# A deformable-convolution and attention kernel: one channel block of the first two chunks' depthwise taps as TensorE products, and TensorE's opening work in another order

## The chip, the cores and the metric

The kernel runs on one core of a Trainium2 chip. A core has five engines, each with its own queue of instructions: PE (TensorE, matrix products; its weight loads are listed as PEld), DVE (VectorE), ACT (ScalarE), POOL (GpSimd) and SP (SyncE, which only issues DMAs). Each engine takes its instructions strictly in order, and an instruction waits on semaphores that other engines and DMAs raise. The metric is the device time of one execution in microseconds (us); before the change the median of three runs is 3317.27 us.

## What is computed

Everything is float32. The input `x` has 2 images of 512 channels and 64x64 pixels. Two layers are added to it.

```python
x = x + _L0_conv_ref(_gn(x), ...)      # deformable convolution
x = x + _L1_conv_ref(_gn(x), ...)      # attention over all pixels, batch norm, relu

def _L0_conv_ref(x, ...):              # inp: x with the channels last
    xproj = inp @ in_w + in_b
    x1 = depthwise 3x3 convolution of x + dw_b
    x1 = gelu(layer norm over channels of x1)
    offset = x1 @ off_w + off_b
    mask = softmax((x1 @ mask_w + mask_b).reshape(N, H, W, G, P), -1)
    out = _dcnv3_core(xproj, offset, mask)   # 9 samples per group, bilinear, weighted by mask
    return out @ out_w + out_b
```

`_gn` is a group norm over 32 groups. The change lies in the first layer, nearly all of it in the work ahead of that layer's loop.

## The kernel before

The 512 channels are four blocks (`KB`) of 128 partitions. An image is eight chunks of 8 rows, 512 pixels; the two images make 16 chunks (`NSEQ`). The first layer is a software pipeline over these 16 chunks, in which each chunk passes four stages. Every stage is a Python generator, and each `yield` ends one step of it:

- `project(i)` (line 738) normalizes the chunk's rows with the group norm's scale and bias into the one buffer `xn` (ScalarE, line 762), multiplies them by `in_w` on TensorE (line 772, four tiles `pq` of 128 pixels), copies each tile out on ScalarE into `xj` (line 778, two buffers), and stores it with two DMAs on SP's queue (line 780) into the padded image `xt` in DRAM.
- `features(i)` (line 786) is the depthwise convolution, the layer norm and Gelu. Tap 1 of each channel block is written by ScalarE (line 798); the other eight taps of each block are added by VectorE, one instruction each (line 806). For chunks 0 and 1 the sum over the channels is taken by TensorE with a matrix of ones over four blocks (`p_mean`, line 822), once for the mean and once for the squares; VectorE subtracts (827), takes the reciprocal and scales (842, 843), ScalarE squares (832), takes the root (840) and Gelu (849). `xn` is one buffer, so the rows of chunk 1 can only be written when TensorE and VectorE have read those of chunk 0.
- `weights(i)` (line 857) makes offsets and masks: TensorE multiplies the features (`po`, line 866), VectorE adds the bias (`o`, line 871), ScalarE takes Exp (878), and VectorE builds the 5x5 window weights `aw` in 17 instructions (909, 914). ScalarE then copies `aw` into `at` (919), TensorE transposes it (928), and ScalarE copies it on.
- `sample(i)` (line 946) spreads the weights (`pb`, `bt`, lines 957 and 962), multiplies them with patches of `xt` (`pa`, line 976), which `fetch` (line 934) has loaded on SP's queue, applies `out_w` (`py`, line 996) and adds the input.

The order of all this on each engine is written out by hand. Everything stands under a manual schedule: a call such as `f0(8)` takes eight steps of a stage, and its instructions go to the engines' queues at that point. Ahead of the loop stands **the fill** (lines 1156 to 1213): chunk 0 through `project`, `features` and `weights`, chunk 1 through `project` and `features`, chunk 2 through `project` and the first seven steps of `features`, six of them taps. In it `p0`, `p1`, `p2` are the projections, `f0`, `f1`, `f` the features of chunks 0, 1 and 2, and `v` the weights of chunk 0. Three further pieces of work are placed among them:

- `border()` (line 695): sixteen stores of the negated bias into the border of `xt` for both images, on SP's queue.
- `more()` (line 1151): one step of `image_stats(1)` (line 703), the group-norm statistics of image 1. Its pieces of 256 KB are loaded on POOL's queue into three buffers (the two halves of `early`, and `xraw`; line 714), and a buffer is loaded again when VectorE has taken its statistic (line 727). The fill takes 13 steps, of which the first only loads; the rest of the steps follow in the loop.
- `products` (`value_weights`, line 1124): four products of weights that the second layer needs (line 1129), copied out by ScalarE into a buffer shared with `xj` and stored on SP's queue (line 1134).

After the fill come 14 calls of `period` (line 1025), which interleaves the stages of four chunks, and then `next_to_last` (line 1087) and `last_period`. The second layer, from line 1235, is not touched.

Of the kernel before, what the change touches and what calls it, by code (L numbers as in the profile page):

```python
# [10 lines left out]
F32 = mybir.dt.float32  # L11
I32 = mybir.dt.int32
AF = mybir.ActivationFunctionType
# [5 lines left out]
P = 128  # L19
NB = 2  # L20
C = 512
KB = C // P
H = W = 64
# [6 lines left out]
NP = 9  # L30
GP = G * NP
CH = 512
NCH = S // CH
ROWS = CH // W
# [484 lines left out]
WIN = W + 4  # L519
# [35 lines left out]
def window_path(  # L555
# [3 lines left out]
    nc = tc.nc  # L559
# [8 lines left out]
    wc_d = dram.tile([P, KB, C], F32, name="wvfc")  # L568
# [57 lines left out]
    with ExitStack() as l0:  # L626
# [68 lines left out]
        def border():  # L695
            for n in range(NB):
                for e in (0, 1, WIN - 2, WIN - 1):
                    nc.sync.dma_start(xt_d[n][e], edge[:WIN, :])
                    nc.sync.dma_start(xt_d[n][2 : H + 2, e, :], edge[:H, :])

        gn = {}

# [35 lines left out]
        def project(i):  # L738

            n, ch = divmod(i, NCH)  # L740
            sc, bi = gn[n]
            lo, hi = max(ch * ROWS - 1, 0), min(ch * ROWS + ROWS + 1, H)
            r0 = lo - (ch * ROWS - 1)
            raws = deque()

            def read(kb):
                if i < 3:
                    raws.append(img[kb][:, lo * W : hi * W].rearrange("p (r c) -> p r c", c=W))
                else:
                    t = io.tile([P, ROWS + 2, W], F32, name="raw", bufs=3)  # L750
                    nc.sync.dma_start(t[:, : hi - lo, :].rearrange("p r c -> p (r c)"), x_v[n, :, kb, lo * W : hi * W])
                    raws.append(t[:, : hi - lo, :])

            for kb in range(3):
                read(kb)
            yield
            if ch == 0:
                nc.gpsimd.memset(xn[:, :, 0, :], 0.0)
            if ch == NCH - 1:
                nc.gpsimd.memset(xn[:, :, ROWS + 1, :], 0.0)  # L760
            for kb in range(KB):
                nc.scalar.activation(  # L762
                    xn[:, kb, r0 : r0 + hi - lo, :], raws.popleft(),
                    AF.Identity, bias=bi[:, kb : kb + 1], scale=sc[:, kb : kb + 1],
                )
                if kb + 3 < KB:
                    read(kb + 3)
                yield
            for t in range(ROWS // 2):
                pq = ps.tile([P, C], F32, tag="mm", name="pq")  # L770
                for kb in range(KB):
                    nc.tensor.matmul(  # L772
                        pq, xn[:, kb, 1 + 2 * t : 3 + 2 * t, :].rearrange("p r c -> p (r c)"), in_w[:, kb, :],
                        start=(kb == 0), stop=(kb == KB - 1),
                    )
                yield
                xj = io.tile([P, C], F32, name="xj", bufs=2)
                nc.scalar.copy(xj, pq)
                for r in range(2):
                    nc.sync.dma_start(xt_d[n][2 + ch * ROWS + 2 * t + r, 2 : W + 2, :], xj[r * W : (r + 1) * W, :])  # L780
                yield

        feats = {}
        conv = cv.tile([P, KB, CH], F32, name="conv")

        def features(i):

            a = cv.tile([P, KB, CH], F32, tag="dT", name="conv1", bufs=2) if i == 1 else conv
            def tap_of(kb, tap):
                dy, dx = tap // 3, tap % 3 - 1  # L790
                acc = a[:, kb, :].rearrange("p (r c) -> p r c", c=W)
                src = xn[:, kb, dy : dy + ROWS, max(dx, 0) : W + min(dx, 0)]
                return acc[:, :, max(-dx, 0) : W + min(-dx, 0)], src, dw_w[:, kb, tap : tap + 1]


            for kb in range(KB):
                dst, src, wt = tap_of(kb, 1)
                nc.scalar.activation(dst, src, AF.Identity, bias=dw_b[:, kb : kb + 1], scale=wt)  # L798
                if i != 2 or kb == KB - 1:
                    yield  # L800
            fill = i < 2
            tot = None if fill else sm.tile([P, CH], F32, tag="tot", name="tot")
            for kb in range(KB):
                for tap in (0, 2, 3, 4, 5, 6, 7, 8):
                    dst, src, wt = tap_of(kb, tap)
                    nc.vector.scalar_tensor_tensor(dst, src, wt, dst, ALU.mult, ALU.add)  # L806
                    if tap < 8:
                        yield

                if not fill:  # L810
                    if kb == 0:
                        nc.gpsimd.dma_start(tot, a[:, 0, :])
                    elif kb < KB - 1:
                        nc.gpsimd.dma_start(tot, a[:, kb, :], accum_op=ALU.add)
                    else:
                        nc.vector.tensor_add(tot, tot, a[:, kb, :])
                yield
# [269 lines left out]
        def next_to_last(y, v, m, w):  # L1087

            y(3)
            w(8)  # L1090
            v(4)
            for steps, tiles in ((1, 2), (1, 2), (2, 1), (1, 0)):
                m(2)
                w(steps)
                y(tiles)
            for _ in range(4):
                m(2)
                w(2)
            w(5)
# [24 lines left out]
        def value_weights():  # L1124

            for cb in range(KB):
                pw = ps.tile([P, C], F32, tag="mm", name="pw")
                for kb in range(KB):
                    nc.tensor.matmul(
                        pw, wv[:, kb, cb * P : (cb + 1) * P], wf[kb], start=(kb == 0), stop=(kb == KB - 1)  # L1130
                    )
                t = io.tile([P, C], F32, tag="xj", name="wc_part", bufs=2)
                nc.scalar.copy(t, pw)
                nc.sync.dma_start(wc_d[:, cb, :], t)
                yield

        def output_bias():
# [13 lines left out]
        def more():  # L1151
            next(later, None)

        with tc.manual_schedule():
# [3 lines left out]
            p0()  # L1158
            for kb in range(KB):
                p0()  # L1160
                f0()
            for t in range(4):
                p0(2)
                f0(8)
            border()
            more()
            p1()
            for kb in range(KB):
                p1()
                f1()  # L1170
                if kb == 1:
                    next(products)
                    next(products)
            f0()
            f1(5)
            p1(4)
            f0()
            f1(11)
            f0()
            for _ in range(6):  # L1180
                more()
            p1(4)
            f0(3)
            f1(16)
            next(products)
            fetch(0, 0)
            fetch(0, 1)
            p2()
            v(4)
            for _ in range(3):  # L1190
                more()
            f1()
            v(2)
            f1()
# [3 lines left out]
            f1()  # L1198
            v()
            f()  # L1200
            for _ in range(3):
                more()
            v(3)
            p2(4)
            f1()
            v(4)
            f1(2)
            v(5)
            p2(4)
            next(products)  # L1210
            run(output_bias())
# [23 lines left out]
    with ExitStack() as l1, tc.manual_schedule():  # L1235
# [78 lines left out]
        with ExitStack() as inner:  # L1314
# [565 lines left out]
            for n in range(NB):  # L1880
# [3 lines left out]
                for i in range(NCH // 2):  # L1884
                    if 0 < i < 3 or n and i == 0:
                        k = i + 1 if i else 1
# [164 lines left out]
```

## Time and profile before

| | us |
|---|---|
| median of three runs (lowest, highest) | 3317.27 (3314.47, 3319.29) |
| the profiled execution's own time | 3313.12 |
| its span, first to last instruction | 3311.0 |
| busy in it: PE, PEld, DVE | 3147.5, 2263.1, 2729.3 |
| busy in it: ACT, POOL | 1342.3, 291.7 |
| mean granted TensorE clock | 0.985 |
| first tap of chunk 0 on VectorE (line 806) | starts at 38.14 |
| first tap of chunk 2 on VectorE (line 806) | starts at 141.91 |
| reciprocal of line 842, first and last of 16 | 85.8 and 1039.4 |

The profiled execution is one run of its own; all times of single instructions come from it and count from the start of its span. A line of a timeline gives the start, the duration, the engine, the source line, the operation, output and inputs with their sizes, how many such instructions are merged, and in brackets how long the engine had been idle before and what ended the wait. A product in float32 is two passes of TensorE, so the profile counts two matmuls for one in the code. A line of stretches gives the busy time of each engine in a window, then the granted clock of TensorE, the share of the DMA engines in use and the GB/s that they moved.

### The profile page before, as it was taken

The numbers are of one execution on the slowest core, as the hardware profiler recorded it, in microseconds if no ns is written. First come the engines' busy times: TensorE is split into PE (matmuls) and PEld (weight loads), VectorE is DVE, ScalarE is ACT, GpSimd is POOL, SyncE is SP. The second block draws the span as 40 slices with busy tenths as digits, with TensorE's granted clock in tenths as the row PEclk, the third lists the DMA queues.
The fourth block names the chain that finished last, engine by engine and source line by source line (L and its number), as shares of the span: only waits on it lengthen the run. The fifth ranks groups of instructions, "written<-read, shape, count | busy, mean of one in ns | idle before, by whom it ended". The sixth has DMA issues, their size and how long they took to land. (4 is left out here: it accounts for less than half of the span.)

```text
span 3311.0 us, 38406 instructions
## 1 busy us (share of the span) xinstructions
PE 3147.5 (95%) x14207; PEld 2263.1 (68%) x14207; DVE 2729.3 (82%) x3907; ACT 1342.3 (41%) x1848; POOL 291.7 (9%) x420
## 2 busy tenths in 40 slices
PE   4899999999999899999999999999999999999993
PEld 2455555555555667787787877887777787787782
DVE  7999999999998678986876977968897796886875
ACT  2678888888887533203113112023311202203114
POOL 1100000000000000001001011000001101001022
PEclk9999999999999999999999999999999999999996
DMA  7345543443444268758657677557667758648689
GB/s 240 120 119 156 152 124 113 138 150 109 120 137 140 93 243 277 213 165 234 194 172 207 202 205 202 198 187 252 225 209 202 205 181 235 198 161 235 197 320 370
DMA packets 241236, 629.06 MB, mean 190 GB/s; under 512 B 28528, under 2 KB 45552, under 8 KB 240016
## 3 DMA queue, kind: packets, MB, share of 16 engines
q1 hardware_dynamic: 177952, 413.37, 37.7%
q0 software_dynamic: 51936, 179.86, 20.7%
q10 hardware_dynamic: 11152, 33.30, 2.7%
q8 instruction: 114, 1.87, 0.2%
q14 instruction: 82, 0.67, 0.1%
HBM read 406.61 MB, written 124.91 MB: 161 GB/s over the span
## 5 line engine op out<-in xcount | busy, mean ns | idle before, releaser
L1572 PE MATMUL accy<-tt,v 128*128 128x256 f32 x1944 | 579.2, 380 | 0.7 <-DVE ct L1638 0.6
L1459 ACT ACTIVATE e<-pS 128x1024 f32<-128x1024 f32 x256 | 248.3, 1021 | 746.8 <-PE pS L1454 732.2
L1572 PE MATMUL accx<-e,v 128*128 128x256 f32 x1728 | 454.2, 385 | 0.0
L1572 PE MATMUL accy<-e,v 128*128 128x256 f32 x1728 | 443.5, 379 | 0.0
L1572 PEld LDWEIGHTS accy<-tt,v 128*128 128x128 f32 x1944 | 369.0, 190 | 53.4 <-DVE tt L1530 2.2
L806 DVE SCALAR_TENSOR_TENSOR conv<-xn,L_conv_dw_w_sb,conv 128x504 f32<-128x504 f32 (+1 forms) x512 | 376.8, 744 | 29.1 <-ACT conv L798 15.2
L1572 PEld LDWEIGHTS accx<-e,v 128*128 128x128 f32 x1728 | 320.9, 190 | 116.7 <-issue 77.6
L1572 PEld LDWEIGHTS accy<-e,v 128*128 128x128 f32 x1728 | 328.3, 190 | 44.7
L1530 DVE TENSOR_TENSOR tt<-tt,e 128x512 f32<-128x512 f32 x432 | 298.9, 692 | 14.8
L1529 DVE TENSOR_TENSOR tt<-e 128x256 f32<-128x256 f32 x432 | 180.9, 419 | 135.8 <-PE accy L1572 133.5
L1572 PE MATMUL accx<-tt,v 128*128 128x256 f32 x972 | 289.9, 380 | 1.3 <-DVE tt L1529 1.3
L976 PEld LDWEIGHTS pa<-bt,patch 96*128 96x128 f32 x2048 | 249.5, 196 | 57.2 <-issue 38.5
L976 PE MATMUL pa<-bt,patch 96*128 96x128 f32 x2048 | 253.4, 280 | 7.8 <-issue 4.2
L1454 PE MATMUL pS<-q,keys 64*128 64x512 f32 x1024 | 254.7, 615 | 0.3 <-DVE stats L1799 0.3
L962 ACT COPY bt<-pb 96x1024 f32<-96x1024 f32 x120 | 226.1, 2025 | 44.0 <-PE pb L957 44.0
L772 PE MATMUL pq<-in_w,xn 128*128 128x512 f32 x512 | 233.8, 599 | 4.3 <-ACT xn L762 4.3
L996 PE MATMUL py<-dT,L_conv_out_w_sb 128*128 128x512 f32 x512 | 230.1, 593 | 0.0
L1577 ACT COPY u<-accx 128x256 f32<-128x256 f32 x54 | 20.1, 372 | 478.6 <-PE accx L1572 475.9
L987 ACT COPY dT<-pa 32x256 f32<-32x256 f32 x496 | 179.5, 362 | 60.3 <-PE pa L976 51.6
L1572 PEld LDWEIGHTS accx<-tt,v 128*128 128x128 f32 x972 | 184.6, 190 | 27.7 <-DVE tt L1529 2.7
L866 PE MATMUL po<-om_w_pg,feat 128*128 128x432 f32 x512 | 201.9, 538 | 1.6 <-ACT feat L849 1.6
L996 PEld LDWEIGHTS py<-dT,L_conv_out_w_sb 128*128 128x128 f32 x512 | 95.5, 190 | 114.3 <-issue 107.4
(289 smaller groups left out, 4383.2 us busy)
## 6 DMA issues: line engine op xcount, KB each, us to landing
v<-wv SPq DMA_DIRECT2D x420, 448.0 KB
tot<-e POOLq DMA_DIRECT2D x160, 512.0 KB, 6.8
patch<-xt SPq DMA_DIRECT2D x256, 192.0 KB
wv<-vform SPq DMA_DIRECT2D x48, 512.0 KB
v<-ww SPq DMA_DIRECT2D x54, 448.0 KB
wv<-vsum SPq DMA_DIRECT2D x48, 384.0 KB
xt<-xj SPq DMA_DIRECT2D x128, 128.0 KB
res<-in_x SPq DMA_DIRECT2D x64, 256.0 KB
```

The costliest lines, as they stand in the source:

```text
L772: nc.tensor.matmul(pq, xn[:, kb, 1 + 2 * t : 3 + 2 * t, :].rearrange("p r c -> p (r c)"), in_w[:, kb, :], start=(kb == 0), stop=(kb == KB ...
L806: nc.vector.scalar_tensor_tensor(dst, src, wt, dst, ALU.mult, ALU.add)
L866: nc.tensor.matmul(po[:, : 3 * GP], f[:, kb, t * P : (t + 1) * P], om_w[:, kb].rearrange("p a k g -> p (a k g)"), start=(kb == 0), stop=(k ...
L962: copy(bt[:SN].rearrange("s g q d -> s d (g q)")[:, d0 : d0 + 4, :], pb[:SN])
L976: nc.tensor.matmul(pa[:, p], xp[:SN, p, cb * P : (cb + 1) * P], bt[:SN, 4 * cb : 4 * cb + 4, PX * s + p, :], start=True, stop=True,)
L987: copy(dst, src)
L996: nc.tensor.matmul(py, out_w[:, kb, cb * P : (cb + 1) * P], dT[:, kb, :], start=(kb == 0), stop=(kb == KB - 1))
L1454: nc.tensor.matmul(p[:, a, :], keys[r, i, (2 * u + h) * P : (2 * u + h + 1) * P], c.q[r, qh, :], start=True, stop=True,)
L1459: nc.scalar.activation(e.rearrange("p a q -> p (a q)"), p.rearrange("p a q -> p (a q)"), AF.Exp)
L1529: nc.vector.tensor_sub(t[:, 0], x[:, 1], x[:, 3])
L1530: nc.vector.tensor_add(t[:, 1:3], t[:, 0].unsqueeze(1).to_broadcast([P, 2, HQ]), x[:, 0:3:2])
L1572: nc.tensor.matmul(out, v[:, blk, :], op, start=(first and g == 0), stop=(final and g == NG))
```

## The change

1. For chunks 0 and 1, the last channel block's nine taps leave ScalarE and VectorE. ScalarE makes nine diagonal matrices of the taps (`diagonals`), and TensorE sums nine products of these with shifted windows of `xn` in one PSUM tile (`deep`); ScalarE copies the tile to `conv` and adds the bias. Chunk 2 and all later chunks keep their taps as they were.
2. `deep(0)` stands between the second and the third projected tile of chunk 0, `deep(1)` ahead of the third projected tile of chunk 1.
3. The four weight products are taken later: none among the first steps of chunk 1, one behind the second tile pair of `p1`, one among the first steps of `p2`, one ahead of the last pair of `p2`'s tiles, and the last where it was. The built order puts them on TensorE behind the fourth tile of chunk 1, behind two tiles of `po`, and behind the second and the fourth tile of chunk 2.
4. Twelve of the thirteen `more()` steps go from three places in the fill to one place behind `v(5)`.
5. The border stores go to POOL's queue. The stores of chunk 2's projected tiles and of the weight products go to ScalarE's queue.
6. In `next_to_last` two steps of `weights` go ahead of the loop of four.

```diff
         def border():
             for n in range(NB):
                 for e in (0, 1, WIN - 2, WIN - 1):
-                    nc.sync.dma_start(xt_d[n][e], edge[:WIN, :])
-                    nc.sync.dma_start(xt_d[n][2 : H + 2, e, :], edge[:H, :])
+                    nc.gpsimd.dma_start(xt_d[n][e], edge[:WIN, :])
+                    nc.gpsimd.dma_start(xt_d[n][2 : H + 2, e, :], edge[:H, :])
...
                 for r in range(2):
-                    nc.sync.dma_start(xt_d[n][2 + ch * ROWS + 2 * t + r, 2 : W + 2, :], xj[r * W : (r + 1) * W, :])
+                    queue = nc.scalar if i == 2 else nc.sync
+                    queue.dma_start(xt_d[n][2 + ch * ROWS + 2 * t + r, 2 : W + 2, :], xj[r * W : (r + 1) * W, :])
...
+        convs, diagonal = {}, []
+
+        def diagonals():
+
+            t = sm.tile([P, NP, P], F32, tag="tx", name="diag")
+            for tap in range(NP):
+                nc.scalar.activation(t[:, tap], ident, AF.Identity, scale=dw_w[:, KB - 1, tap : tap + 1])
+            diagonal.append(t)
+
+        def deep(i):
+
+            kb = KB - 1
+            p = ps.tile([P, CH], F32, tag="mm", name="p_dw")
+            to = p.rearrange("p (r c) -> p r c", c=W)
+            for k, tap in enumerate((1, 0, 2, 3, 4, 5, 6, 7, 8)):
+                dy, dx = tap // 3, tap % 3 - 1
+                nc.tensor.matmul(
+                    to[:, :, max(-dx, 0) : W + min(-dx, 0)], diagonal[0][:, tap],
+                    xn[:, kb, dy : dy + ROWS, max(dx, 0) : W + min(dx, 0)], start=(k == 0), stop=(k == NP - 1),
+                )
+            nc.scalar.activation(convs[i][:, kb, :], p, AF.Identity, bias=dw_b[:, kb : kb + 1])
+
         def features(i):
...
+            convs[i] = a
+            direct = range(KB - 1) if i < 2 else range(KB)
...
-            for kb in range(KB):
+            for kb in direct:
...
             y(3)
             w(8)
             v(4)
-            for steps, tiles in ((1, 2), (1, 2), (2, 1), (1, 0)):
+            w(2)
+            for steps, tiles in ((1, 2), (1, 2), (0, 1), (1, 0)):
...
-                nc.sync.dma_start(wc_d[:, cb, :], t)
+                nc.scalar.dma_start(wc_d[:, cb, :], t)
...
             for kb in range(KB):
                 p0()
-                f0()
-            for t in range(4):
+                if kb < KB - 1:
+                    f0()
+            diagonals()
+            for k in range(4):
                 p0(2)
-                f0(8)
+                if k == 1:
+                    deep(0)
+                if k < 3:
+                    f0(8)
             border()
             more()
             p1()
             for kb in range(KB):
                 p1()
-                f1()
-                if kb == 1:
-                    next(products)
-                    next(products)
+                if kb < KB - 1:
+                    f1()
             f0()
             f1(5)
             p1(4)
             f0()
             f1(11)
             f0()
-            for _ in range(6):
-                more()
+            deep(1)
             p1(4)
             f0(3)
-            f1(16)
+            f1(8)
             next(products)
             fetch(0, 0)
             fetch(0, 1)
             p2()
             v(4)
-            for _ in range(3):
-                more()
+            next(products)
             f1()
...
             f()
-            for _ in range(3):
-                more()
             v(3)
...
             v(5)
+            next(products)
+            for _ in range(12):
+                more()
             p2(4)
             next(products)
```

More of the change, by code (lines that the diff above doesn't have):

```diff
@@ L802, in features @@
             tot = None if fill else sm.tile([P, CH], F32, tag="tot", name="tot")
-            for kb in range(KB):
+            for kb in direct:
                 for tap in (0, 2, 3, 4, 5, 6, 7, 8):
```

## The prediction

> **What bounds the kernel now.** The change touches the opening of the first layer (to about 142 us) and five steps near that layer's end. I read the page's slices first, then busy time by stretches, then the timelines of VectorE, ScalarE and TensorE from 36 to 235 us, then the order in which the changed kernel's instructions stand on each engine. From the page:
>
> ```profile
> PE   4899999999999899999999999999999999999993
> ...
> DVE  7999999999998678986876977968897796886875
> ```
>
> A slice is 83 us. In the first layer, the first 14 slices or so, both engines are nearly full, so a start that comes later has nowhere to be made good. By stretches (length, then busy time of PE, PEld, DVE, ACT, POOL, then clock and DMA):
>
> ```profile
> 50.00:100.00 50.00, 41.71 (x93) 17.59 (x92) 43.83 (x54) 20.67 (x27) 4.58 (x7) 0.93 0.45 122
> 100.00:150.00 50.00, 41.67 (x146) 22.85 (x145) 45.51 (x58) 28.91 (x37) 5.73 (x9) 0.90 0.46 146
> ...
> 200.00:250.00 50.00, 48.66 (x237) 28.47 (x236) 46.83 (x65) 40.20 (x56) 5.92 (x8) 1.00 0.46 134
> ```
>
> In the fill VectorE is the fuller engine and TensorE has some 8 us free in each 50. VectorE's timeline there:
>
> ```profile
> 77.18 1.28 DVE L727 BATCH_NORM_STATS2 gn_st<-early 128x6 f32<-128x512 f32 x2
> 78.38 0.68 DVE L727 BATCH_NORM_STATS2 gn_st<-xraw 128x6 f32<-128x512 f32 x1
> 82.57 0.69 DVE L727 BATCH_NORM_STATS2 gn_st<-early 128x6 f32<-128x512 f32 x1 [3.51 <-DMA early<-in_x]
> ...
> 108.15 0.61 DVE L871 TENSOR_TENSOR o<-po,om_b_pg 128x432 f32<-128x432 f32 x1 [1.09 <-PE po L866]
> ...
> 118.45 1.14 DVE L893 TENSOR_REDUCE sx<-o 128x64 f32<-128x576 f32 x1 [2.15 <-ACT o L878]
> ...
> 141.84 0.15 DVE L1145 TENSOR_TENSOR L_conv_out_b_sb<-L_conv_out_b_sb,p_bias 128x4 f32<-128x4 f32 x1
> 141.91 4.64 DVE L806 SCALAR_TENSOR_TENSOR conv<-xn,L_conv_dw_w_sb,conv 128x504 f32<-128x504 f32 x6
> ```
>
> The last line matters most: at 141.91 VectorE begins the taps of chunk 2, the first work of the loop. From there it is idle only 2.5 us up to 209 (1.06, 0.63 and 0.82), so **the number to find is when that line starts after the change.** Beside it, ScalarE and TensorE:
>
> ```profile
> 54.12 0.92 ACT L762 ACTIVATE xn<-bt,gn_bias,gn_scale 128x640 f32<-128x640 f32 x1
> 75.88 1.22 ACT L778 COPY xj<-pq 128x512 f32<-128x512 f32 x2 [11.14 <-DMA wvfc<-wc_part]
> 92.81 4.96 ACT L849 ACTIVATE feat<-conv,L_conv_ln_b_sb,L_conv_ln_g_sb 128x512 f32<-128x512 f32 x4
> ```
> ```profile
> 101.61 3.60 PE L822 MATMUL p_mean<-conv,ones_c 128*128 128x512 f32 x8
> 105.05 5.96 PE L866 MATMUL po<-om_w_pg,feat 128*128 128x432 f32 x16
> 115.20 13.90 PE L772 MATMUL pq<-in_w,xn 128*128 128x512 f32 x32
> ```
>
> **What goes.** VectorE loses 16 taps. 31 of them take 23.68 us, 0.764 each, so 12.2 us. ScalarE's 11.14 us wait goes, as the 16 border stores leave SP's queue. Both were worth having only if VectorE then has something to do.
>
> **What comes, along the new chain.** Each block by TensorE is nine products of two passes. 32 passes took 13.90 us (0.434 each), so 18 passes are 7.8 us. Four projected tiles left ScalarE at 43.29, 46.73, 50.20 and 53.64, 3.45 us each.
> 1. The order puts block 0 behind the second tile, so the fourth moves from 53.64 to 61.4. The rows that it frees are rewritten behind it in ScalarE's queue: the xn row at 54.12 becomes 61.9 and the first tap of chunk 1 is written at 63.7. VectorE ends its 24 taps of chunk 0 at 38.14 + 24 x 0.766 + 0.34 = 56.9 and **sits idle 6.8 us**. Five taps and the 2.28 us subtraction end at 69.8.
> 2. ScalarE writes the other rows of xn at 1.72 us each (54.12 to 55.84), to 68.0. Two tiles behind that end at 72.3, the copy at 72.9, the four squares (2.19) at 75.1, their mean at 76.0.
> 3. Block 1 stands next: 83.8. Two tiles more: 90.7, copy 91.3. ScalarE's table load (1.28) and Gelu stand behind that copy: **Gelu of chunk 0 at 92.6, against 92.81 before.** What the removed wait and taps gave, the two blocks have taken (2 x 7.8).
> 4. Before, the mean of chunk 1 started at 101.61, 3.8 us after Gelu's end. Now a weight product (8 passes, 3.6 us by the rows of 3.60) stands ahead of it: 105.0, **3.4 late**. The sums `o`, the squares, Exp, `sx`, the softmax and the 17 `aw` instructions all follow from it. VectorE's idle time there (1.09, 2.15) grows, since the statistics that filled it are gone. `aw` ends at 141.9 + 3.4 = 145.3.
> 5. The order puts the twelve statistics behind `aw` and ahead of the taps of chunk 2. No such run of twelve is in the trace. From below, with no wait: 12 x 0.64 + 0.37 = 8.05. There are three buffers, so three are loaded ahead and each later set needs a round trip: statistic 0.69, semaphore 0.05, POOL's issue 0.54, landing 3.1 (the median of the loads into `early`; `xraw` has 5.6), in all 4.4. Three of these and the last set (1.9 + 0.37) make 15.5. From above, by the round trip seen from 77.18 to 82.57, 5.4, three times and the same last set: 18.5. I take 15.5, nearest to the load's own row.
> 6. The bias add, then the taps: 145.3 + 15.5 + 0.1 = 160.9 against 141.91: **+19.0 us.**
>
> [...]
>
> **What costs nothing, and its cover.** Nine diagonal weights on ScalarE: between the rows of 128x4 (0.30) and 128x512 (0.81), so 2.7 to 7.3 us in all; TensorE uses one each 0.87 us and starts 4 us later, so it does not wait. POOL issues 16 stores (0.54 each, 9 us) ahead of its loads and the `aw` memset; it was idle 42 us there and the first user is at 128. ScalarE issues 12 DMAs (0.45 each, 5.4 us); the eight of the tiles reuse semaphores held by the patch loads, which took SP 14.40 us. Queued behind them are Gelu of chunk 1, then `at`. The statistics cover this: up to 15 us late, `at` still comes before VectorE is free. In the next-to-last period two weight steps move ahead of two patch products; VectorE waits 1.67 to 9.91 us in places there (1061 to 1111 us), so I take 0, bounds -1 and +1.
>
> **Does the loop give any back?** `at` starts some 3 us late and VectorE 19 us late. But the taps feed the mean, the squares and, through the period's order, the next `aw`; TensorE will idle in the first period where it now waits 0.75 to 2.00 us. The 2.5 us of VectorE idle follow its own results. I take nothing back; at most 2.5.
>
> **Sum.** The profiled execution took 3313.1 us (span 3311.0 and 2.1 around it), 4.2 under the median of 3317.3. 3313.1 + 19.0 = 3332.1 for a like execution, **3336 on the median.** Low end: statistics without waits (-7.45) and 2.5 absorbed: +9.0, 3326. High end: statistics at 18.5 (+3.0), and the blocks' passes, which read runs of 63 and were never seen, at 0.68 as in the slow row of 77.68 to 83.12 (5.44 us for 8): 36 x 0.25 = +9: +31, 3348.
>
> **Rivals.**
> - *Faster: TensorE's blocks are hidden.* VectorE is the fuller engine, and if Gelu came when ScalarE's wait allowed, VectorE would save 12.2 us and up to its 8.1 us of idle (3.51, 1.31, 1.09, 2.15): 3297 to 3305. It decides at step 3: without 12.2 us of taps and 4.8 of idle VectorE reaches the `o` sums at 86.6 instead of 103.6, so Gelu (4.96, then 0.9 for a tile) would have to start by about 80, not 92.6. Against: both blocks and four tiles stand ahead of it in ScalarE's queue. 0.07.
> - *No measurable change: the loop waits for the `at` chain, not for the taps.* TensorE is 48.66 of 50 busy in the loop, for it. Then only step 4's 3.4 us stays: 3321. Against: the same period has TensorE idle behind VectorE's `tot` and `feat`. 0.08.
> - *Worse: ScalarE's queue hangs on the patch loads,* with 14.40 us of patches and 10.57 of tile stores, longer than the statistics cover: 5 to 12 us more, 3341 to 3348. 0.07.
> - *Forecast,* 3326 to 3348: 0.78.
>
> The range 3321 to 3348 takes in the second and third rival. About 0.2% (6.6 us) is what a measurement here can tell from no change: faster is the first rival, 0.07; within 0.2% the second, 0.08; slower 0.85.
>
> **What would show it.** VectorE idle about 7 us near 57; Gelu of chunk 0 near 92.6; the mean of chunk 1 near 105; twelve statistics in a row from about 145 to 161 with waits for `early` and `xraw`; the first tap of chunk 2 near 161; TensorE idle over 10 us in the first period; equal spacing of the later periods (`rstd` each 65.6 us). A Gelu before 85, or statistics that end before 150, would make it wrong.

## The result, and the profile after

The changed kernel takes 3333.05 us in the median of five runs (3331.53 to 3339.59), the kernel before 3317.27 in five runs beside them (3311.67 to 3319.29). By the medians it is slower by 15.8 us. The ratio on record is 1.0056, with a 95% interval of 1.0046 to 1.0067, which is 15 to 22 us; it is formed from the runs in another way than as the quotient of the two medians, which is 1.0048. The forecast was 3336 us.

The profiled execution is the slowest of the five, 3339.59 us with a span of 3337.8. From its page, the slices of TensorE and VectorE:

```profile
PE   5979999999999999999999999999999999999993
...
DVE  7599999999999668986886976968897696885875
```

The only clear losses are in the second and third slice, that is, up to 250 us: VectorE falls from 9 to 5 in the second, TensorE from 9 to 7 in the third. What the later slices lose is too little for tenths to show. By stretches of the same trace (length, then busy time of PE, PEld, DVE, ACT, POOL, then clock and DMA):

```profile
50.00:100.00 50.00, 47.51 (x111) 20.27 (x110) 31.45 (x36) 20.02 (x26) 4.53 (x7) 1.00 0.31 78
100.00:150.00 50.00, 46.12 (x129) 24.75 (x128) 31.44 (x35) 25.89 (x34) 1.61 (x3) 0.92 0.39 125
150.00:200.00 50.00, 32.96 (x177) 21.90 (x176) 44.25 (x63) 27.25 (x33) 10.25 (x16) 0.81 0.29 90
```

Before, VectorE was busy 43.83 and 45.51 us in the first two stretches and TensorE 41.71 and 41.67. The change turned that round: TensorE is now the full engine, at 47.51 and 46.12, and VectorE has 37 us to spare. In the third stretch TensorE stands 17 us, behind VectorE. VectorE's timeline of the changed kernel shows where (start, duration, and in brackets the idle time before it and what ended it):

```profile
62.46 3.87 DVE L832 SCALAR_TENSOR_TENSOR conv<-xn,L_conv_dw_w_sb,conv 128x504 f32<-128x504 f32 x5 [6.80 <-ACT conv L824]
...
98.61 0.61 DVE L897 TENSOR_TENSOR o<-po,om_b_pg 128x432 f32<-128x432 f32 x1 [9.98 <-PE po L892]
...
111.28 0.61 DVE L897 TENSOR_TENSOR o<-po,om_b_pg 128x432 f32<-128x432 f32 x1 [9.16 <-PE po L892]
...
121.58 1.14 DVE L919 TENSOR_REDUCE sx<-o 128x64 f32<-128x576 f32 x1 [3.93 <-ACT o L904]
...
144.97 1.28 DVE L727 BATCH_NORM_STATS2 gn_st<-early 128x6 f32<-128x512 f32 x2
146.16 0.68 DVE L727 BATCH_NORM_STATS2 gn_st<-xraw 128x6 f32<-128x512 f32 x1
150.12 1.40 DVE L727 BATCH_NORM_STATS2 gn_st<-early 128x6 f32<-128x512 f32 x2 [3.28 <-DMA early<-in_x]
...
160.58 0.69 DVE L727 BATCH_NORM_STATS2 gn_st<-xraw 128x6 f32<-128x512 f32 x1 [0.76 <-DMA xraw<-in_x]
161.19 0.14 DVE L1172 TENSOR_TENSOR L_conv_out_b_sb<-L_conv_out_b_sb,p_bias 128x4 f32<-128x4 f32 x1
161.25 4.64 DVE L832 SCALAR_TENSOR_TENSOR conv<-xn,L_conv_dw_w_sb,conv 128x504 f32<-128x504 f32 x6
```

Two things are to be seen. The waits for `po`, 1.09 us before, are now 9.98 and 9.16 with nothing put into them. And the statistics that used to fill such waits stand in one row from 144.97 to 161.19, each group behind the DMA that loads its buffer. The first tap of chunk 2 starts at 161.25, where it was 141.91. From ScalarE and TensorE, the lines for the steps of the prediction:

```profile
92.56 4.91 ACT L875 ACTIVATE feat<-conv,L_conv_ln_b_sb,L_conv_ln_g_sb 128x512 f32<-128x512 f32 x4
...
135.55 1.28 ACT L875 ACT_TABLE_LOAD   x1 [5.07 <-DMA patch<-xt]
...
147.55 2.94 ACT L945 COPY at<-aw 128x400 f32<-128x400 f32 x4 [0.45 <-ACT wc_part L1160]
```
```profile
45.37 7.81 PE L803 MATMUL p_dw<-xn,diag 128*128 128x512 f32 x18
...
104.75 3.60 PE L848 MATMUL p_mean<-conv,ones_c 128*128 128x512 f32 x8
...
189.43 2.07 PE L848 MATMUL p_mean<-tot,ones_c 128*128 128x512 f32 x2 [14.15 <-DVE tot L842]
```

The last line answers for the loop: in its first period TensorE waits 14.15 us for VectorE.

### The profile page after: what moved, and what is told of

It is laid out like the page before. It is cut to its first block, busy times and chain, and to the rows that moved or that the text cites. A ratio compares the mean times of both kernels' runs of the same rounds, so it can differ in the third digit from the quotient of the medians.

```text
span 3337.8 us, 38479 instructions
## 1 busy us (share of the span) xinstructions
PE 3174.1 (95%) x14243; PEld 2277.8 (68%) x14243; DVE 2719.4 (81%) x3891; ACT 1344.7 (40%) x1857; POOL 300.6 (9%) x436
## 5 line engine op out<-in xcount | busy, mean ns | idle before, releaser
L832 DVE SCALAR_TENSOR_TENSOR conv<-xn,L_conv_dw_w_sb,conv 128x504 f32<-128x504 f32 x496 | 365.1, 744 | 37.9 <-ACT conv L824 24.4
L892 PE MATMUL po<-om_w_pg,feat 128*128 128x432 f32 x512 | 210.3, 557 | 0.7 <-ACT feat L875 0.7
```

Source lines behind the costliest of these rows:

```text
L892: nc.tensor.matmul(po[:, : 3 * GP], f[:, kb, t * P : (t + 1) * P], om_w[:, kb].rearrange("p a k g -> p (a k g)"), start=(kb == 0), stop=(k ...
```

## The experiments

The theory after the result: the row of statistics costs most, and the blocks cost the rest, because TensorE has become the full engine of the fill. The rivals: that the order of Gelu and of the weight products is what costs; that the moved queues cost; that the blocks save after all. Twelve runs. For each, the table gives the median with the number of runs, the ratio to the kernel before on the same chip, and from its profiled execution the time from the first tap of chunk 0 to the first tap of chunk 2 (the fill) and to the third `rstd` reciprocal (the first in the loop). These two are counted from that first tap because it starts up to 1.5 us earlier in some kernels than in the kernel before. It does so in the seven kernels (the change, e1, e3 to e6, e8) in which the first three statistics loads of image 1 stand behind the border stores on POOL's queue: there they are issued after 52 us, and the first tap starts at 36.62 to 37.11. In the other seven they are issued at 2.7 us, in the middle of the first loads of the kernel, and the tap starts at 37.86 to 38.44. That these loads take the time is likely, but was not tried by itself.

| kernel | us (runs) | ratio [95%] | fill | to third rstd |
|---|---|---|---|---|
| before | | 1 | 103.8 | 147.8 |
| the change | 3333.05 (5) | 1.0056 [1.0046, 1.0067] | 124.3 | 168.4 |
| e1_stats_back | 3323.46 (10) | 1.0014 [1.0004, 1.0025] | 115.0 | 159.1 |
| e2_stats_alone | 3331.10 (7) | 1.0036 [1.0024, 1.0047] | 121.0 | 165.1 |
| e3_no_blocks | 3329.09 (6) | 1.0037 [1.0023, 1.0051] | 118.4 | 162.5 |
| e4_queues_alone | 3321.42 (10) | 1.0012 [1.0002, 1.0022] | 103.7 | 149.4 |
| e5_mean_first | 3330.28 (4) | 1.0055 [1.0040, 1.0070] | 123.7 | 167.8 |
| e6_gelu_first | 3330.85 (4) | 1.0053 [1.0038, 1.0067] | 123.3 | 167.4 |
| e7_one_block_spread | 3312.86 (11) | 0.9999 [0.9990, 1.0008] | 94.0 | 150.1 |
| e8_bias_behind_taps | 3321.51 (8) | 1.0025 [1.0015, 1.0035] | 108.0 | 157.4 |
| e9_best | 3307.13 (10) | 0.9978 [0.9968, 0.9988] | 94.0 | 140.0 |
| e10_best_no_block | 3315.62 (11) | 1.0002 [0.9993, 1.0011] | 98.0 | 144.2 |
| e11_best_act_stores | 3315.36 (11) | 0.9998 [0.9989, 1.0007] | 94.1 | 147.3 |
| e12_best_two_blocks | 3313.73 (11) | 0.9988 [0.9979, 0.9997] | 101.1 | 146.7 |

The kernel before had a median of 3316.91 beside e1 to e4, 3313.70 beside e5 to e8, 3315.74 beside e9 to e11 and 3316.58 beside e12.

**e1, the statistics back in their three places.**

```diff
             deep(1)
+            for _ in range(6):
+                more()
             p1(4)
...
             next(products)
+            for _ in range(3):
+                more()
             f1()
...
             f()
+            for _ in range(3):
+                more()
             v(3)
...
-            for _ in range(12):
-                more()
```

> The changed kernel with its twelve statistics put back at the three places that they had before; all else as changed. Theory (the statistics in one row ahead of chunk 2's taps are most of the loss): the 16.2 us from 144.97 to 161.19 leave the path, and what returns of them lies in VectorE's waits of 9.98, 9.16 and 3.93 us; 12 to 16 us less than the changed kernel's 3333, so 3317 to 3321. First tap of chunk 2 about 108 to 112 us behind the first tap of chunk 0 (changed: 124.3, before: 103.8). Rival (the loss is TensorE's two blocks, 2 x 7.8 = 15.6 us, and the statistics only fill time in which VectorE waits anyway): no change, 3330 to 3335.

The fill falls by 9.3 us, and the ratio from 1.0056 to 1.0014. The time stays 2.5 us above the expected range, and the trace says why: with the row gone, VectorE waits for the next thing. VectorE in e1:

```profile
152.02 0.16 DVE L1172 TENSOR_TENSOR L_conv_out_b_sb<-L_conv_out_b_sb,p_bias 128x4 f32<-128x4 f32 x1 [6.36 <-PE p_bias L1168]
```

The bias waits for TensorE, TensorE for ScalarE's copy of a weight product, and ScalarE for DMAs. ScalarE in e1:

```profile
132.73 0.59 ACT L778 COPY xj<-pq 128x512 f32<-128x512 f32 x1 [4.15 <-DMA patch<-xt]
...
138.24 1.28 ACT L875 ACT_TABLE_LOAD   x1 [4.92 <-DMA xt<-xj]
```

Some 3.3 of VectorE's 6.36 us go with TensorE's clock. TensorE in e1:

```profile
145.00 6.99 PE L1168 MATMUL p_bias<-L_conv_in_b_sb,L_conv_out_w_sb 128*128 128x1 f32 x32 [5.29 <-ACT wc_part L1160]
```

Behind an idle time of 5.29 us these 32 passes took 6.99 us, at a granted clock of 0.50 (145 to 152 us). In the kernel before, with no wait ahead of them, they took 3.66 us at 0.98 (132.4 to 136 us). In the changed kernel they took 6.99 us as well, behind an idle time of 3.22 us and at 0.50 (142.3 to 149.3 us), but under the row of statistics.

**e2, item 4 of the change alone:** the kernel before, with the twelve `more()` calls moved behind `v(5)`.

> The kernel before with the twelve statistics alone moved to their new place, ahead of the last two tiles of chunk 2; nothing else changed. Theory: VectorE was the full engine, the statistics took 8.05 us of it and 4.8 us of waits for their loads, of which it saves at most the 4.8 and some filled waits; in one row they cost about 16: 9 to 15 us more than before, 3326 to 3332. Rival (blocks): within 3 us of before, 3314 to 3320.

The theory holds: the row alone puts 17.2 us on the fill. So the single parts do not add up: 17.2 alone, but only 9.3 when taken from the whole change, since there the row also hides ScalarE's waits: with the row gone, VectorE still stands 6.36 us for the bias.

**e3, the change without the two blocks** (`direct = range(KB)`, and no `diagonals` or `deep`).

> The changed kernel without the two blocks: all taps of chunks 0 and 1 stay with ScalarE and VectorE; the order of weight products, statistics and queues as changed. Theory: TensorE loses 15.6 us, VectorE gets 12.2 us back, and the row of statistics stays: 6 to 11 us less than the changed kernel, 3322 to 3327, so the blocks are a loss by themselves and the smaller part. Rival (blocks are the whole loss): 3315 to 3319. Third account (the blocks gain what VectorE saves, the order loses): 3340 or more.

The fill is 5.8 us shorter without them, and the ratio goes from 1.0056 to 1.0037. The time is 2 us above what was expected. So in this order the blocks cost something: the fill says it, while the two intervals overlap slightly.

**e4, item 5 alone:** the kernel before, with the border stores on POOL's queue and the stores of chunk 2 and of the products on ScalarE's.

> The kernel before with the queues alone changed: border stores on POOL's queue, the stores of chunk 2's tiles and of the weight products on ScalarE's. Theory: ScalarE's wait of 11.14 us near 65 us goes, but VectorE had work in it, so little moves: -3 to +3 us, 3314 to 3320. Rival (ScalarE's queue hangs on the patch loads): 5 us or more above before, with a wait for patch loads on ScalarE ahead of the copies of line 945's counterpart, and the first tap of chunk 2 later than 103.8 us behind the first tap of chunk 0 by as much.

The fill does not move (103.7). ScalarE does wait for patch loads, 3.56 us at a tile copy, and the copy of `aw` comes at 143.82; the third `rstd` is 1.6 us later. The time is 1.4 us above the first range and does not reach the 5 us of the rival, with an interval that begins at 1.0002. In the profiled executions, 7.7 of the 9.5 us between e4 and the kernel before lie in the loop, with five of the slowed product groups that the last section describes. So what item 5 costs by itself stays open.

**e5, the mean of chunk 1 ahead of the weight product.**

```diff
             p2()
             v(4)
-            next(products)
             f1()
             v(2)
             f1()
             v(2)
+            next(products)
             p2(4)
```

> The changed kernel with the second weight product moved from ahead of the mean of chunk 1 to behind it (ahead of chunk 2's projected tiles). The prediction's step 4 put 3.4 us of delay on this product. If that is right, the mean of chunk 1 starts at about 101.2 instead of 104.8, the first tap of chunk 2 at about 157.8 instead of 161.2, and the time falls by some 3.4 us, to 3329.6. My theory now is that TensorE is the fuller engine from 50 to 150 us, so that the same products only change places: the mean comes 3.6 us earlier, but the product then delays what stands behind it, the first tap of chunk 2 moves by less than 1.5 us, and the time stays within 3330 to 3334.

The mean starts at 102.13 instead of 104.75, and yet the fill shortens by only 0.6 us. TensorE's products change places and their sum stays: the mean of the squares, which stands behind them, starts at 114.80 in both traces.

**e6, Gelu of chunk 0 first.**

```diff
             f0()
+            f0(3)
             deep(1)
             p1(4)
-            f0(3)
             f1(8)
```

> The changed kernel with the reciprocal, the scaling and Gelu of chunk 0 ahead of the second TensorE block and the third projected tile of chunk 1. The prediction's first rival (faster) was said to decide at Gelu's start: Gelu near 84 instead of 92.6. If Gelu's place is what costs, the sums o, the softmax and aw follow 8 us earlier, the first tap of chunk 2 is near 153, and the time is near 3325. If TensorE's sum of work decides (two blocks of 7.8 us, none removed), Gelu starts near 84 but the block, the tiles and the mean of chunk 1 that stand behind it come later by as much as it saved; the first tap of chunk 2 moves by 1 to 3 us, and the time is 3330 to 3333.

Gelu starts at 83.98 instead of 92.56, 8.6 us earlier, and the fill shortens by 1.0 us. What Gelu gained stands in TensorE's queue again behind the block, the tiles and a product.

**e7, one block, and the work spread.**

```diff
                     xn[:, kb, dy : dy + ROWS, max(dx, 0) : W + min(dx, 0)], start=(k == 0), stop=(k == NP - 1),
                 )
+            yield
             nc.scalar.activation(convs[i][:, kb, :], p, AF.Identity, bias=dw_b[:, kb : kb + 1])
+            yield
...
-            direct = range(KB - 1) if i < 2 else range(KB)
+            direct = range(KB - 1) if i in (0,) else range(KB)
...
             diagonals()
+            d0 = deep(0)
+            more()
             for k in range(4):
                 p0(2)
-                if k == 1:
-                    deep(0)
                 if k < 3:
                     f0(8)
-            border()
-            more()
+            next(d0)
+            for _ in range(3):
+                more()
             p1()
-            for kb in range(KB):
+            for kb in range(KB - 1):
                 p1()
-                if kb < KB - 1:
-                    f1()
+                f1()
+            next(d0)
+            p1()
+            f1()
...
             f0()
-            deep(1)
-            p1(4)
+            border()
             f0(3)
-            f1(8)
-            next(products)
+            p1(4)
+            f1(13)
+            for _ in range(3):
+                more()
...
             next(products)
-            run(output_bias())
+            next(products)
             f(6)
+            run(output_bias())
```

Lines that only take the same steps in other portions are left out. The other six statistics stand in two groups of three, behind the Exp of chunk 0 and behind `v(3)`. Of the four products one goes behind Exp and three behind `v(5)`.

> The best order that the traces suggest: one TensorE block only (chunk 0), issued behind the fourth tile of chunk 0 and copied out behind the xn rows of chunk 1, so that no row of xn waits for ScalarE's copy; chunk 1 keeps its taps on VectorE; Gelu of chunk 0 ahead of the third tile of chunk 1; the twelve statistics in four groups of three where VectorE waits; the border stores later on POOL; the weight products last; the bias add behind the six taps of chunk 2. If the cost was the row of statistics and the waits that the order makes, the first tap of chunk 2 comes 5 to 7 us earlier after the start of chunk 0's taps than before the change (97 to 99 us instead of 103.8), and the time is 3309 to 3313, under both kernels. If ScalarE's waits for the patch loads (up to 15 us together, without the cover of the statistics) or TensorE's added 7.8 us decide, the first tap is at 104 or later and the time is 3317 to 3322.

Half of this came true. The fill is 9.8 us shorter than before the change, more than expected, and yet the time is that of the kernel before: the third `rstd` is 2.3 us later. What VectorE won, it then waits for. VectorE in e7:

```profile
132.16 4.64 DVE L834 SCALAR_TENSOR_TENSOR conv<-xn,L_conv_dw_w_sb,conv 128x504 f32<-128x504 f32 x6
144.30 0.16 DVE L1174 TENSOR_TENSOR L_conv_out_b_sb<-L_conv_out_b_sb,p_bias 128x4 f32<-128x4 f32 x1 [7.49 <-PE p_bias L1170]
...
155.13 0.61 DVE L899 TENSOR_TENSOR o<-po,om_b_pg 128x432 f32<-128x432 f32 x1 [4.26 <-PE po L894]
```

ScalarE waits 5.00 and 3.58 us for patch loads and tile stores, and copies `aw` into `at` at 143.06, although `aw` was ready at 132.25.

**e8, the statistics as in e1, and the bias add behind the taps** (`f(6)` ahead of `run(output_bias())`).

> The changed kernel with the statistics back in their three places (as in the run before) and the addition of the output bias on VectorE moved behind the six taps of chunk 2. With the statistics back VectorE stood 6.36 us ahead of those taps for the bias, which waits for weight products that ScalarE copies late because its queue waits for patch loads. If that wait was the next limit, the first tap of chunk 2 comes 6 us earlier (fill 109 instead of 115 us), and the time is 3317 to 3320, against 3323.5. If the limit is ScalarE's queue itself (the copies of aw behind the same waits), the taps come earlier but the third rstd reciprocal of the loop does not, and the time stays at 3322 to 3325.

The first tap of chunk 2 comes 7.0 us earlier and the third `rstd` only 1.7. The time does not fall by anything that can be told: the ratios of e1 and e8 overlap, and 3321.51 lies between the two expected ranges. The trace speaks for the second: `aw` ends at 144.83, and ScalarE's queue copies it only at 148.39.

**e9, the version that beats both kernels:** e7 with what its trace asks for.

```diff
-                    queue = nc.scalar if i == 2 else nc.sync
+                    queue = nc.sync
...
-                nc.scalar.dma_start(wc_d[:, cb, :], t)
+                nc.sync.dma_start(wc_d[:, cb, :], t)
...
             f0(3)
             p1(4)
+            next(products)
             f1(13)
...
-            fetch(0, 0)
-            fetch(0, 1)
             p2()
             v(8)
...
             v(5)
             next(products)
             p2(4)
-            next(products)
-            next(products)
             f(6)
+            v(4)
+            fetch(0, 0)
+            fetch(0, 1)
+            next(products)
             run(output_bias())
-            v(4)
```

> The spread order of the run before (one TensorE block, statistics in VectorE's gaps), with what its trace asks for: the stores of chunk 2's tiles and of the weight products back on SP's queue, the patch loads of chunk 0 issued behind those stores instead of ahead of them, the copy of aw into at ahead of the last weight product and of the bias, and one weight product earlier, where TensorE waited 2.4 us for Gelu. My theory: the spread order had won 9.8 us of fill, and ScalarE's queue, hanging on patch loads (5.00, 3.58 and 3.84 us), had lost them again, since the copy of aw came at 143.1 instead of 132.3. Then the copy comes within 1 us of the end of aw, VectorE does not wait for the bias or for po, the third rstd comes 6 to 8 us earlier after the first tap of chunk 0 than before the change (140 to 142 us instead of 147.8), and the time is 6 to 9 us under the kernel before: 3305 to 3310. Rival: TensorE's added 7.8 us are what is given back (TensorE is full in the fill); then the third rstd stays at 147 to 150 and the time within 3 us of the kernel before.

The first expectation came, but for a wait of 1.75 us for `po` at 145.34: 3307.13 us, 8.6 under the kernel before, ratio 0.9978 with an interval that ends at 0.9988. ScalarE and TensorE in e9:

```profile
132.64 3.00 ACT L947 COPY at<-aw 128x400 f32<-128x400 f32 x4 [4.86 <-DVE aw L942]
```
```profile
136.13 1.97 PE L956 MATMUL p_tr<-ident,at 128*128 128x128 f32 x8 [0.36 <-ACT wc_part L1162]
```

The copy of `aw` now follows VectorE, whose `aw` ends at 132.56, and TensorE goes on with hardly a wait. By stretches, e9 has both engines nearly full in the fill:

```profile
50.00:100.00 50.00, 48.55 (x118) 21.82 (x118) 43.92 (x56) 21.43 (x28) 13.17 (x23) 1.00 0.43 112
100.00:150.00 50.00, 48.96 (x173) 26.00 (x173) 47.03 (x59) 34.23 (x41) 7.22 (x11) 0.90 0.48 150
```

**e10, e9 without its block** (`direct = range(KB)`, no `diagonals` or `deep`; `f0` and `f1` with all their steps).

> The same order without any TensorE block: all four channel blocks of chunks 0 and 1 on VectorE as before the change. It tells what the block itself is worth. By the rows, 8 taps of 0.766 us leave VectorE and 7.8 us come to TensorE. If VectorE sets the end of the fill in this order, the third rstd comes 4 to 6 us later than with the block, and the time is 3310 to 3315. If TensorE sets it, the time is that with the block or 2 to 5 us under it.

The third `rstd` is 4.1 us later, the time 8.5 us above e9's and that of the kernel before. So in this order one block is worth something; the same order without it is worth nothing that can be measured. Only 4.1 us of the 8.5 are seen in the fill: VectorE is rid of eight taps (6.1 us) and has two new waits behind TensorE's sums (1.52 and 0.43 us). The loop of the profiled execution of e10 took 4.7 us more than e9's, with five slowed product groups against three (last section). So 4.1 us is what the block is shown to be worth, and the rest need not be its doing.

**e11, e9 with item 5 of the change again:** the stores on ScalarE's queue and the patch loads issued ahead of them.

> The same order as the first run of this call, with one thing undone: the stores of chunk 2's tiles and of the weight products are on ScalarE's queue, as in the change, and the patch loads are issued ahead of them, as in both kernels. If ScalarE's queue hanging on the patch loads is what cost the gain, ScalarE waits 3.5 to 5 us at the tile copies and at Gelu's table load of chunk 1, the copy of aw comes 6 to 10 us after the end of aw, and the time is 5 to 8 us above the first run, near the kernel before: 3311 to 3316. If the order of the copy and the products was the cause, the time is that of the first run.

As the first expectation has it. VectorE's `aw` ends at 132.00, and ScalarE in e11 copies it 7.7 us later:

```profile
122.22 0.59 ACT L778 COPY xj<-pq 128x512 f32<-128x512 f32 x1 [4.83 <-DMA patch<-xt]
...
137.93 0.59 ACT L778 COPY xj<-pq 128x512 f32<-128x512 f32 x1 [3.75 <-DMA xt<-xj]
...
139.74 2.98 ACT L947 COPY at<-aw 128x400 f32<-128x400 f32 x4 [1.23 <-issue]
```

The fill is as short as e9's, and all of the gain is gone: 8.2 us. The queue and the place of the loads were undone together; which of the two costs more was not tried.

**e12, e9 with the second block as well** (`direct = range(KB - 1) if i < 2 else range(KB)`, `deep(1)` ahead of `f0(3)`, its copy behind it).

> The best order so far with the second TensorE block of the change put back: chunk 1's last channel block also goes to TensorE, its nine products behind the projected tiles 1 and 2 of chunk 1, its copy on ScalarE behind Gelu of chunk 0. VectorE loses 8 more taps (6.1 us), TensorE gains 7.8 us. In the order with one block TensorE had only 1.2, 0.2 and 0.4 us of waits left between 64 and 138 us, so my theory is that the second block pushes Gelu's products and all behind them back by nearly its length: fill 101 us instead of 94, third rstd 147 us after the first tap instead of 140, the time 5 to 8 us above the order with one block, 3311 to 3316. Rival: VectorE's 6.1 us still set the end, as they did for the first block; then the time is at or under that with one block, 3301 to 3308.

The second block takes back 6.7 us up to the third `rstd`, as the first expectation has it, and the time is 3313.73. The ratios say it less sharply: 0.9988 against 0.9978, with intervals that overlap. VectorE in e12, at the sums of chunk 0:

```profile
97.39 0.61 DVE L899 TENSOR_TENSOR o<-po,om_b_pg 128x432 f32<-128x432 f32 x1 [8.87 <-PE po L894]
```

e9 waits 0.57 us at this place. What VectorE saves by the second block, and more, it spends waiting for TensorE.

## Why the prediction was right, and where it was not

*What bounds it.* The start of chunk 2's taps was the number to find, and it was. The two columns of the table show its limit too: once the fill is shorter than before (e7, e11), the copy of `aw` on ScalarE sets the end, and the third `rstd` is the better guide to the time. It is not exact: in e10 it comes 3.6 us earlier than before the change, and the time is the same.

*What goes* (ScalarE's wait of 11.14 us): gone, its longest from 43 to 77 us is 7.06, for `p_dw`. Before, the border stores held SP's queue from 55.43 to 71.47, and the stores of the weight products, on which it waited, came behind them, at 71.57. *Step 1* (VectorE idle 6.8 us): 6.80. *Steps 2 and 3* (Gelu of chunk 0 at 92.6): 92.56, but by two errors that cancel. The whole chain started 1.2 us earlier than assumed, and the mean of the squares of chunk 0 ended 2.2 us behind the last square (73.87 to 76.07), where step 2 put 0.9. The blocks' passes took 7.81 us for 18, as the row of 0.434 each gave; the windows that read runs of 63 showed no slower pass, so that part of the upper end can go.

*Step 4* (the mean of chunk 1 at 105.0, `aw` ends at 145.3): 104.75 and 145.05. The times are right, the cause is not. The step laid the 3.4 us on one weight product that stands ahead of the mean. e5 took it away, and `aw` ended at 144.85. What delays is the sum of TensorE's work: any one product moved is replaced by another.

*Step 5* (statistics, 15.5 us, taken from the round trip of a load): 16.2 in the trace, 17.6 in e2. The three round trips took 13.0 us (144.97 to 158.01) where 13.2 were forecast, the last set 3.2 where 2.3 were, since its three pieces landed one after the other. No row shows the term of 0.05 for the semaphore: from the start of a statistic to the start of POOL's next load the rows before had 0.99 us (82.57 to 83.56), not 0.74. *Step 6* (first tap of chunk 2 at 160.9, +19.0): 161.25, +19.3. The number is right by the help of an offset: the changed kernel starts the taps of chunk 0 at 36.98, 1.16 us earlier, which was not foreseen (e4 shows it with the queues alone, 37.11), and the fill from there is 20.5 us longer, 1.5 more than forecast. That the two nearly cancel is luck.

*What costs nothing.* ScalarE's 12 DMAs were costed at nothing under the cover of the statistics. That holds, with the cover: in the changed kernel the copy of `aw` starts at 147.55, 2.5 us behind the end of `aw` and 13.7 ahead of chunk 2's taps. But a price lies beneath: 8.2 us in e11, where the cover is gone, for the queue and the place of the loads together. The steps in `next_to_last` were not tried alone; from the sixteenth `rstd` to the end the profiled executions took 2271.6 us before and 2270.8 after.

*The loop gives nothing back.* The third `rstd` is at 205.33 against 185.97, +19.4. Right. But "equal spacing of the later periods" failed in the profiled execution: its 13 periods took 861.7 us against 853.5, which goes with a slower clock, told in the last section.

*The sum.* +19.0 was forecast, the medians show +15.8, the ratio's interval +15 to +22 us. The profiled executions differ by more, 26.8 in their spans: 19.4 up to the third `rstd` and 8.2 in the 13 periods, less 0.8 behind them. The changed kernel's other four runs are 6 to 8 us under its profiled one.

*The rivals.* "Faster" was said to decide at Gelu's start, by about 80. e6 brought Gelu to 84, two thirds of the way, and gained 1.0 us, while e9 is the faster kernel with Gelu at 84.50. So the condition was wrong: not Gelu's place but TensorE's sum with two blocks decides. With one block and the gaps filled (e9) the same mechanism does make the kernel faster, by 8.6 us, less than the 12 to 20 that this rival named. "The `at` chain" was no bound of the changed kernel, but it is the bound of e7 and e11. "ScalarE's queue hangs on the patch loads" is shown to exist (5.07 us above) and to cost nothing there: its condition, a wait longer than the statistics, was not met.

## What to carry to other kernels

When work moves from the fuller engine to the other, add up both engines over the whole path that is to become shorter, not over a fixed stretch. By the stretch from 50 to 150 us, TensorE had 16.6 us free before, and two blocks (15.6 us) would have fitted. Over the fill, TensorE and VectorE are busy 88.9 and 92.5 of 98.0 us in e10, 92.3 and 86.8 of 94.0 in e9, and 99.4 and 81.2 of 101.1 in e12: with one block TensorE is already the fuller engine and nearly without waits, so the second lengthens the fill by almost its own length (7.1 of 7.8 us). Small pieces such as statistics belong in the waits of their engine; in a row they cost their own time and the round trip of every buffer as well (here 16.2 us for twelve of 0.64 to 0.69). Look beneath a cover before costing an edit at nothing: a queue that waits for DMAs on an engine that also computes shows its price only when the work that hid it has gone (8.2 us in e11).

## What the runs showed of the hardware

TensorE was slowed for a few microseconds in the middle of the loop, where it is nearly always busy (49.16 of the 50 us from 250 to 300 in the changed kernel), in some executions and not in others. TensorE in the changed kernel's trace, and the stretches around it:

```profile
364.38 3.17 PE L892 MATMUL po<-om_w_pg,feat 128*128 128x432 f32 x8
367.47 1.10 PE L983 MATMUL pb<-awT,sel 25*96 25x256 f32 x8
369.05 1.11 PE L983 MATMUL pb<-awT,sel 25*96 25x256 f32 x8 [0.47 <-ACT bt L988]
370.08 4.86 PE L892 MATMUL po<-om_w_pg,feat 128*128 128x432 f32 x8
```
```profile
363.80:367.20 3.40, 3.40 (x20) 1.63 (x12) 3.29 (x5) 3.40 (x5) 0.54 (x1) 1.00 0.73 238
367.20:370.60 3.40, 2.93 (x18) 1.45 (x18) 3.29 (x6) 3.40 (x4) 0.00 (x0) 0.98 0.98 328
370.60:374.00 3.40, 3.40 (x6) 1.66 (x5) 3.26 (x6) 2.06 (x2) 1.36 (x2) 0.52 0.36 137
374.00:377.40 3.40, 3.40 (x23) 1.71 (x22) 3.13 (x5) 1.37 (x1) 0.09 (x1) 1.00 0.70 158
```

Eight passes of `po` that take 3.17 us took 4.86, under a clock of 0.52 in one stretch of 3.4 us. It happened five times in this execution, at the same group of products each time (370.08, 503.21, 636.01, 834.46 and 967.40), three times in e9's and never in the loop of the execution before. Five times 1.69 are 8.5 us; the 13 periods took 8.2 more than before. All fourteen profiled executions bear it out: in each, the 13 periods take 853.5 us and 1.69 for every such group, to within 1.8 us. There is none before and in e5 (853.5 and 853.6 us), one in e2 (855.5), three in e1, e3, e8, e9 and e11 (857.1 to 860.3), four in e6 and e7 (860.3 and 859.9), and five in the change, e4, e10 and e12 (860.4 to 861.8). The runs without a profile have only their mean clock on record, and their times go with it: the ten of e9 run from 3299.36 us at 0.987 to 3312.80 at 0.983. So much of the scatter between the runs of one kernel goes with the granted clock; where in those runs it fell, no record shows.

The work just ahead does not tell a slowed group from another in this trace. In the 3.4 us ahead of the stretch at 0.52 TensorE was busy 2.93 us, mostly with products that read 25 partitions (`pb`, 2.2 us). In the 3.4 us ahead of the group at 238.04 (234.60 to 238.00) it was busy 2.94 us with the same products, and that group took 3.17 us at a clock of 1.00. What sets the slowing off, and why in some periods only, no run shows.
